# A two-block attention convolution on one core: group norm by single chunks, tile work of a pair's first image in the second attention, m2 and cv1's sums moved, first pair reordered

## The chip, the cores and the metric

The kernel runs on one core of a Trainium2 chip, in float32 throughout. The metric is the device time of one execution in microseconds (us), as the median of several runs. A profiled execution gives, for each engine, every instruction with its start and length. The engines are TensorE (PE in the profile; its weight loads are PEld), VectorE (DVE), ScalarE (ACT), GpSimd (POOL) and SyncE (SP), which issues most of the DMAs; GpSimd issues the others.

## The reference

Eight images of 512 channels and 32 x 32 pixels are normalised by groups of 16 channels and sent through a block with a residual around it. Cut to what matters:

```python
t = cbs(gn(x), cv1_w, cv1_bn, 0)            # 1x1 conv 512 -> 512, batch norm, silu
ys = [t[:, :256], t[:, 256:]]
for i in range(2):
    yi = ys[-1]
    z = cbs(yi, m_cv1_w[i], m_cv1_bn[i], 1)  # 3x3 conv 256 -> 256
    q, k, v = 1x1 conv of z, 256 -> 768      # 4 heads of 64, 1024 positions
    a = softmax(q . (k + rw + rh) / 8)
    z = silu(bn(1x1 conv of (a . v)))        # "m2" in the kernel
    ys.append(yi + z)
out = x + cbs(concat(ys), cv2_w, cv2_bn, 0)  # 1x1 conv 1024 -> 512
```

## The kernel before

The images go in four pairs (p = 0 to 3). Channels lie on the 128 partitions, so an image of 512 channels is four chunks of 128 x 1024. Within a pair the stages of block 0 are: the 3 x 3 conv of both images; projection of the first image to q, k, v; its attention (the *first attention*); a *middle* stage; projection of the second image; its attention (the *second attention*); m2 and the tiles of the second image. Block 1 follows with the same stages, and cv2 at the end of each image.

**The 3 x 3 conv** is a Winograd form. `tiles_in` (L453) makes its input side on VectorE from the padded image in `Y1` or `Y2`, in three steps i = 0, 1, 2, each of some 14 VectorE operations and two GpSimd memsets; a step's first tiles use the tag "acc", of which there are two buffers and which the attention's sums also use. The filters' side, `make_u` (L352), is made once at the start and in pair 0 (nine steps for each quarter of a filter, through `step_u`), stored to DRAM through GpSimd's queue and loaded back through SP's.

**Projection** is `project_strassen` (L737): seven products instead of eight, of sums of z (`first_sum`, t1 to t4), with the results combined on VectorE. PSUM has three "big" buffers and one "av" buffer. A `middle` function can be called inside it, in the kernel before after the fourth product; block 1 and pair 3 call m2 there.

**Attention** (`attention_fast`, L837) walks four groups of 8 key tiles in pairs of tiles: two logits matmul groups (`l_ps`, L860), two exps on ScalarE (`pt`, L864, six buffers of tag "pt"), sums of the exps on VectorE (`acc`, L878 and L880), and the products with v (`av_ps`, L894), which ScalarE (L901) and VectorE (L902) evict at a group's end. `sums`, `spread` and `scale` send the row sums through DRAM and multiply z by their reciprocals (L966). Foreign work is put in by `behind`, a table from (group, step) to a function; `hooks` fills it with `step_norm`, at the steps listed in `NORMS`, and `step_u`.

**Group norm** of the next pair's images (`group_norm`, L666) runs in such steps: statistics of two chunks, of the other two, the group means, then rstd, shift and all eight applications (L687, halves of a chunk) in one step.

**cv1** of the next pair's images is spread around the attentions as `begin`, `go_on`, `sums`, `rest(0)` to `rest(3)`, `adds`, `adds2`, `finish` and `keep`. In pair 0 (`direct`) it is a plain product by output chunk; later pairs use a Strassen form.

**The middle stage** (L1588) of pairs 0 to 2 is: cv1's second part and sums, `spread`, `scale`, m2 of the first image (which writes `Y2[0]`), the rest of cv1, then `tiles_in` of `Y2[0]` with results `v_new` put in tag "pt" and stored to DRAM by GpSimd, the next loads of x, and the projection of the second image. Pair 3 has no cv1: it calls m2 inside the projection and does the tile steps in the second attention, at the steps (0, 2), (1, 2) and (2, 2), with v_new in tag "x".

**The start** (L1372 to L1465) computes the norm of the first two images, filters (0, 1) and (0, 0), cv1 of both images, `make_sq` (sums for the projection's weights) and the tiles, with `issue_after` setting parts of the order. `load_bottleneck` (L174) loads m2's weights and makes r = rw + rh (`r_new`) on GpSimd for both blocks. Each engine executes its instructions in order; that order comes from a scheduler that honours `issue_after`.

Of the kernel before, what the change touches and what calls it, by code (L numbers as in the profile page):

```python
# [61 lines left out]
def kernel(  # L62
# [70 lines left out]

    xs = [load_x(act, 0, c, NX) for c in range(NX // 2)]
# [28 lines left out]

    xs_second = []
# [6 lines left out]
    m2_sb = const.tile([P, N, NM, C], F32, name="m2_sb")  # L171
    rw_sb = const.tile([P, N, NM, F], F32, name="rw_sb")
    rh_sb = const.tile([P, N, NM, F], F32, name="rh_sb")

    def load_bottleneck(n):
        raw = act.tile([P, NM, F], F32, tag="t", name="rw_raw", bufs=4)
        nc.sync.dma_start(raw, m_rw[n].rearrange("(k p) f -> p k f", p=P))
        nc.sync.dma_start(rh_sb[:, n], m_rh[n].rearrange("(k p) f -> p k f", p=P))
        nc.sync.dma_start(m2_sb[:, n], m_cv2_w[n].rearrange("(k p) o -> p k o", p=P))
        nc.gpsimd.tensor_copy(planes(rw_sb[:, n]), natural(raw))  # L180
        for c in range(NM):
            for half in range(NH):
                r = act.tile([P, ROWS, F], F32, tag="t", name="r_new", bufs=4)
                nc.gpsimd.tensor_tensor(
                    r, rw_sb[:, n, c].unsqueeze(1).to_broadcast([P, ROWS, F]),
                    rh_sb[:, n, c, ts(half, ROWS)].unsqueeze(2).to_broadcast([P, ROWS, F]), ALU.add,
                )
                nc.gpsimd.dma_start(r_dram[n][c][:, ts(half, HALF)], r.rearrange("p h w -> p (h w)"))
# [236 lines left out]
    def stages(act, small, ps_big, ps_av, n_pt):  # L425
# [219 lines left out]
        def group_norm_part(xts):  # L645
# [3 lines left out]
            for c in range(n):  # L649
                gn_stats(mv, c, xts[c])  # L650
# [15 lines left out]
        def group_norm(xts):  # L666

            mv = small.tile([P, NX, 2], F32, tag="mv", name="mv", bufs=2)

            def stats(cs):  # L670
                for c in cs:
                    gn_stats(mv, c, xts[c])

            stats(range(NX // 2))
            yield
            stats(range(NX // 2, NX))
            yield
# [5 lines left out]
            nc.gpsimd.tensor_scalar(shift, shift, -1.0, None, ALU.mult)  # L683
            for c in range(NX):
                for half in range(NH):
                    part = xts[c][:, ts(half, HALF)]
                    nc.scalar.activation(part, part, AF.Identity, scale=gr[:, c : c + 1], bias=shift[:, c : c + 1])  # L687
            yield
# [48 lines left out]
        def project_strassen(n, z, w, t, early=None, middle=None):  # L737
# [64 lines left out]
            if middle:  # L802
                middle()
# [3 lines left out]
            tt(u_v, ps_w[:, 0], u_v, ALU.add)  # L807
            ps_d = big()
# [617 lines left out]
    with tc.issue_after(last.ins), tc.issue_after(applied.ins):  # L1426
        norm = s.group_norm_part(xs_second)
# [3 lines left out]
    areas[0, 0, 0] = load_raw(0, 0, 0, Y2[0])  # L1431
    areas[0, 0, 1] = load_raw(0, 0, 1, Y2[1])
# [13 lines left out]
    for n in range(N):  # L1446
        load_bottleneck(n)
    scratch = act.tile([P, 4, HW], F32, tag="z", name="sq_new")
    flat = scratch.rearrange("p a b -> p (a b)")
    tiles = [flat[:, ts(k, 3 * C)] for k in range(NM)]  # L1450
    load_qkv(0, tiles)
    sums = [flat[:, 2 * 3 * C + j * 3 * P : 2 * 3 * C + (j + 1) * 3 * P].rearrange("p (w o) -> p w o", w=3) for j in range(4)]
    with tc.issue_after(made.ins):
        made = make_sq(0, tiles, sums)
# [4 lines left out]
    with tc.issue_after(made.ins):  # L1459
        ecs = [{}, {}]  # L1460
        for i in range(NI):
            for g in range(G):
                s.tiles_in(Y1[g], putter(vs, g), [i], ecs[g])
# [3 lines left out]
    for p in range(NP):  # L1467
# [23 lines left out]
        def next_cv1(which, xts, y1, b):  # L1491
# [3 lines left out]
            if direct:  # L1495
# [4 lines left out]
                    rest=lambda i: one(1 + i) if i in (1, 2) else None, adds=nothing, adds2=nothing, finish=nothing,  # L1500
# [46 lines left out]
        def hooks(norms, every=1):  # L1547
            calls = {}
            for g in range(NG):
                for at in range(4):  # L1550
                    key = (g, at) if at else g
                    calls[key] = [step_norm] if key in norms else []
                    if (4 * g + at) % every == 0:
                        calls[key].append(step_u)
            return {key: (lambda fs: lambda: [f() for f in fs])(fs) for key, fs in calls.items()}

        NORMS = (1, 2, (2, 2), 3)
# [14 lines left out]
        def put_away(i, cp):  # L1572
            tag, bufs = ("pt", 6) if more else ("x", NX)
            v_new[i, cp] = t = act.tile([P, 2, 2 * P], F32, tag=tag, name="v_new", bufs=bufs)
# [13 lines left out]
        if more:  # L1588
# [4 lines left out]
            nxt.rest(0)  # L1593
            end.scale()
            last = m2_a()
            for i in range(1, 4):
                nxt.rest(i)
            with tc.issue_after(last.ins):
                t = s.first_sum(z[:, :, 1])
                nxt.adds()  # L1600
# [5 lines left out]
            for i in range(2):  # L1606
                s.tiles_in(Y2[0], put_away, [i], ec)
                store(i)
            for _ in range(12):
                step_u()  # L1610
# [5 lines left out]
            s.tiles_in(Y2[0], put_away, [2], ec)  # L1616
            store(2)
        else:
            norm = None
            t = s.first_sum(z[:, :, 1])  # L1620

            def middle():
                end.spread()
                end.scale()
                m2_a()
                with tc.issue_after(s.silu_in[-1].ins):
                    s.table_of(AF.Exp)

            feed(units(1)[:6])
            qkv = s.project_strassen(  # L1630
                0, z[:, :, 1], take_blocks("sq", 0, 1, SQ_NAMES), t, early=end.sums, middle=middle
            )

            def tiles_later(i):
                s.tiles_in(Y2[0], put_away, [i], ec)
                store(i)
# [11 lines left out]
        behind = hooks(NORMS) | {NG: begin_cv1(1, Y1[1], ia + 3), NG + 1: lambda: nxt.go_on()}  # L1648
        if not more:
# [11 lines left out]
            behind |= {(i, 2): (lambda i: lambda: tiles_later(i))(i) for i in range(NI)}  # L1661
# [231 lines left out]
```

## Time and profile before

| What | us |
|---|---|
| median of 3 runs (2430.92 to 2432.46) | 2432.45 |
| profiled execution | 2428.35 |
| its span, first to last instruction | 2426.9 |
| TensorE busy | 2253.8 |
| VectorE busy | 1776.7 |
| ScalarE busy | 1100.2 |
| mean granted TensorE clock | 0.973 of full |

TensorE's first attention matmul starts at 163.55 us. The block 0 part of pair 0 lasts until 485.6 (conv of block 1 included), pair 1 starts its first attention at 786.7, pair 2 at 1368.6, pair 3 at 1950.9. A row of a timeline reads: start, length, engine, line and operation, output and inputs, shape, number of instructions, and in brackets the idle time of that engine before it with the instruction that ended the wait.

### The profile page before, as it was taken

To read this page: it belongs to the slowest core of one execution; us is meant where nothing else is said; L and a number is where in the kernel's file an instruction comes from. 1 tells how busy PE (TensorE), PEld (TensorE's weight loads), DVE (VectorE), ACT (ScalarE), POOL (GpSimd) and SP (SyncE) were. 2 spreads that over 40 slices of the span, in tenths; PEclk is the share of its full clock that TensorE was granted. 3 is DMA by queue.
4 is the path that set the end of the run, shared out by engine and by line. 5 is a ranking of instruction groups with operands and counts; after the bars stand their busy time and mean duration, and the time that the engine had idled before them with its cause. 6 is when DMAs were issued, how large, how long until landed. Compare 5 with 4: busy or idle time off the path is not lost.

```text
span 2426.9 us, 40682 instructions
## 1 busy us (share of the span) xinstructions
PE 2253.8 (93%) x16378; PEld 1092.5 (45%) x16378; DVE 1776.7 (73%) x2678; ACT 1100.2 (45%) x1341; POOL 214.7 (9%) x435
## 2 busy tenths in 40 slices
PE   6798788999999989999999998999999999999997
PEld 2462333734447343554346534373434734373433
DVE  7987585877857768786884858698685777797652
ACT  4245344365323655446522565535642355435532
POOL 5201110000021000000012001000002100000002
PEclk9899889999999999999999999999999999999999
DMA  8631623621257041443137414161215712251205
GB/s 309 243 125 67 239 76 96 242 91 59 57 154 246 17 161 49 162 128 97 32 87 225 143 58 152 59 215 54 88 45 131 254 36 71 83 178 35 75 17 137
DMA packets 137477, 290.89 MB, mean 120 GB/s; under 512 B 34656, under 2 KB 63824, under 8 KB 136256
## 3 DMA queue, kind: packets, MB, share of 16 engines
q1 hardware_dynamic: 108976, 201.29, 25.7%
q0 software_dynamic: 28304, 86.92, 11.7%
q8 instruction: 131, 2.15, 0.4%
q14 instruction: 66, 0.54, 0.1%
HBM read 216.97 MB, written 71.17 MB: 119 GB/s over the span
## 4 chain that ended last, share of the span: by engine, by line
PE 51%; DVE 21%; issue 17%; DMA 5%; ACT 4%; POOL 2%; SPq 0%; DVEq 0%; ACTq 0%; POOLq 0%
PE av_ps L894 12%; PE l_ps L860 12%; PE p_ps L750 5%; PE c L1111 5%; PE m_ps L1091 3%; PE c_new L1111 3%; PE ps L448 3%; DVE acc L880 3%; PE x_ps L1211 2%; PE c_ps L565 2%; DMA c_out<-in_x_dram 2%; PE pv_ps L756 2%; ACT x L687 1%; ACT pt L864 1%; DVE c_e L573 1%
## 5 line engine op out<-in xcount | busy, mean ns | idle before, releaser
L864 ACT ACTIVATE pt<-l_ps 128x1024 f32<-128x1024 f32 x512 | 495.9, 1022 | 373.6 <-PE l_ps L860 339.3
L880 DVE TENSOR_TENSOR acc<-acc,pt 128x1024 f32<-128x1024 f32 x384 | 469.8, 1223 | 128.7 <-ACT pt L864 104.5
L860 PE MATMUL l_ps<-q,kr 64*64 64x512 f32 x4096 | 494.2, 598 | 44.4 <-ACT pt L864 43.0
L894 PE MATMUL av_ps<-pt,vT 64*64 64x512 f32 x4096 | 500.1, 606 | 11.2 <-DVE z L902 7.6
L860 PEld LDWEIGHTS l_ps<-q,kr 64*64 64x64 f32 x4096 | 157.5, 134 | 316.8 <-issue 245.3
L894 PEld LDWEIGHTS av_ps<-pt,vT 64*64 64x64 f32 x4096 | 157.4, 136 | 300.0 <-issue 256.2
L565 PE MATMUL c_ps<-v_in,u 128*64 128x128 f32 x4320 | 239.9, 273 | 5.2 <-issue 2.7
L565 PEld LDWEIGHTS c_ps<-v_in,u 128*64 128x64 f32 x4320 | 235.8, 137 | 12.8 <-issue 12.8
L750 PE MATMUL p_ps<-t_z,sq 128*128 128x512 f32 x256 | 126.2, 609 | 7.6 <-DVE c_t L572 7.6
L1091 PE MATMUL m_ps<-z,m_sb 128*128 128x512 f32 x256 | 114.3, 599 | 7.9 <-DVE z L966 7.9
L750 PE MATMUL p_ps<-z,sq 128*128 128x512 f32 x192 | 97.9, 645 | 24.3 <-ACT u_z L784 14.9
L570 ACT COPY c_m<-c_ps 128x512 f32<-128x512 f32 x48 | 28.1, 586 | 174.8 <-PE c_ps L565 110.0
L878 DVE TENSOR_TENSOR acc<-pt 128x1024 f32<-128x1024 f32 x64 | 78.2, 1221 | 30.4 <-ACT pt L864 30.4
L966 DVE TENSOR_TENSOR z<-z,rs 128x512 f32<-128x512 f32 x64 | 44.1, 689 | 68.3 <-DMA rs<-r_dram 68.0
L429 ACT ACTIVATE t<-m_ps,bh,sh 128x512 f32<-128x512 f32 x64 | 46.9, 776 | 81.3 <-PE m_ps L1091 80.9
L1091 PEld LDWEIGHTS m_ps<-z,m_sb 128*128 128x128 f32 x256 | 48.7, 192 | 67.6 <-issue 57.2
L1161 POOL DMA_DIRECT2D c_out<-in_x_dram x56 | 49.6, 967 | 307.8 <-ACT c_out L429 303.2
L756 PE MATMUL pv_ps<-sq,z 128*128 128x128 f32 x384 | 54.1, 285 | 16.0 <-DVE z L902 8.2
L756 PEld LDWEIGHTS pv_ps<-sq,z 128*128 128x128 f32 x384 | 50.3, 196 | 40.2 <-DVE z L902 11.3
L750 PEld LDWEIGHTS p_ps<-z,sq 128*128 128x128 f32 x192 | 36.4, 204 | 67.9 <-issue 39.5
L750 PEld LDWEIGHTS p_ps<-t_z,sq 128*128 128x128 f32 x256 | 44.9, 195 | 42.3 <-issue 32.3
L902 DVE TENSOR_TENSOR z<-av_ps,z 128x512 f32<-128x512 f32 x64 | 44.1, 689 | 24.3 <-ACT z L901 24.3
(278 smaller groups left out, 3149.9 us busy)
## 6 DMA issues: line engine op xcount, KB each, us to landing
u<-u SPq DMA_DIRECT2D x135, 512.0 KB
sq<-sq SPq DMA_DIRECT2D x48, 384.0 KB
r_in<-r SPq DMA_DIRECT2D x32, 512.0 KB
rs<-r_dram SPq DMA_DIRECT2D x120, 128.0 KB
x<-in_x_dram SPq DMA_DIRECT2D x28, 512.0 KB
y_in<-y SPq DMA_DIRECT2D x28, 512.0 KB
c_out<-in_x_dram POOLq DMA_DIRECT2D x56, 256.0 KB, 5.3
out_dram<-c_out POOLq DMA_DIRECT2D x56, 256.0 KB, 3.2
```

The costliest lines, as they stand in the source:

```text
L448: last_product[0] = nc.tensor.matmul(ps[:, half, :], w_of(k), rhs_of(k, half), start=(k == begin), stop=(k == end))
L565: nc.tensor.matmul(to[o], us[cp][:, k, row, c, o], rhs, start=(k == 0), stop=(k == NM - 1),)
L750: nc.tensor.matmul(ps[:, o, :], w[:, o, :], rhs, start=not onto, stop=True, skip_group_check=onto)
L756: nc.tensor.matmul(v[:, ts(j, P)], rhs[:, ts(j, P)], w[:, 2, :], start=j == 0 and not onto, stop=True, skip_group_check=True,)
L860: nc.tensor.matmul(ps[kh * HD : (kh + 1) * HD, hd, :], kr[r, c, o : o + HD], q[r, c, ts(half, HALF)], start=True, stop=True,)
L864: exp = nc.scalar.activation(pt, ps, AF.Exp, scale=SCALE)
L878: return nc.vector.tensor_tensor(accs[g], pt[0], pt[1], ALU.add)
L880: ins = nc.vector.tensor_tensor(accs[g], accs[g], pt[i], ALU.add)
L894: nc.tensor.matmul(avs[g][hd * HD : (hd + 1) * HD, kh, :], vT[r, j, o : o + HD], pt[i][r, hd, :], start=(j == 0), stop=(j == NJ - 1),)
L1091: nc.tensor.matmul(pss[oc][:, half, :], m2_sb[:, n, k, ts(oc, P)], ao[:, k, ts(half, HALF)], start=(k == 0), stop=(k == NM - 1),)
L1111: nc.tensor.matmul(ps[:, o, :], w[:, k, ts(o, P)], rhs[part][:, c], start=(k == 0 and not onto), stop=(k == KB - 1), skip_group_check=onto,)
L1161: nc.gpsimd.dma_start(t, rows_of(x, i, at), accum_op=ALU.add)
```

## The change

- `group_norm` gives one chunk per step, for statistics and for application, and applies a whole chunk in one activation. `NORMS` has ten steps.
- The tiles of a pair's first image move for all pairs to the second attention, at (0, 2), (1, 2), (2, 2), with v_new in tag "t" (four buffers).
- `middle` is called after the fifth product (s2) of `project_strassen`.
- In the middle stage of pairs 1 and 2 `rest(1)` and `adds` come before m2. Pair 0 goes pair 3's way: m2 and two output chunks of cv1 inside the projection.
- At the start, the second image's statistics come from ScalarE (`stats_by_act`), the filter (0, 0) is loaded earlier into the tile of z (`load_taps`), r of block 0 is made early and that of block 1 after pair 0's projection, the qkv weights go to `Y2`, `make_sq` comes after the tiles, and the tiles' order changes.

```diff
-    def load_bottleneck(n):
+    def load_r(n):
         raw = act.tile([P, NM, F], F32, tag="t", name="rw_raw", bufs=4)
         nc.sync.dma_start(raw, m_rw[n].rearrange("(k p) f -> p k f", p=P))
         nc.sync.dma_start(rh_sb[:, n], m_rh[n].rearrange("(k p) f -> p k f", p=P))
+        return raw
+    rw_raw = load_r(0)
+    taps = act.tile([P, NM, 2 * HW], F32, tag="z", name="taps")
+    areas[0, 0, 0] = load_taps(0, 0, 0, taps[:, 0])
     xs_second = []
...
+    areas[0, 0, 1] = load_taps(0, 0, 1, taps[:, 1])
+    def load_m2(n):
         nc.sync.dma_start(m2_sb[:, n], m_cv2_w[n].rearrange("(k p) o -> p k o", p=P))
+    def make_r(n, raw):
         nc.gpsimd.tensor_copy(planes(rw_sb[:, n]), natural(raw))
...
+        def stats_by_act(mv, xts):
+            n = len(xts)
...
+            def each(func, to, **kw):
+                for c in range(n):
+                    bias = {k: v[:, c : c + 1] for k, v in kw.items()}
+                    junk = act.tile([P, HW], F32, tag="acc", name="junk", bufs=2)
+                    nc.scalar.activation(junk, xts[c], func, accum_out=to[:, c : c + 1], **bias)
+            each(AF.Identity, total)
+            nc.vector.tensor_scalar(mean, total, -1.0 / HW, None, ALU.mult)
+            each(AF.Square, square, bias=mean)
+            nc.vector.tensor_scalar(mv[:, :, 0], total, 1.0 / HW, None, ALU.mult)
+            nc.vector.tensor_scalar(mv[:, :, 1], square, 1.0 / HW, None, ALU.mult)
...
         def group_norm(xts):
             mv = small.tile([P, NX, 2], F32, tag="mv", name="mv", bufs=2)
-            def stats(cs):
-                for c in cs:
-                    gn_stats(mv, c, xts[c])
-            stats(range(NX // 2))
-            yield
-            stats(range(NX // 2, NX))
-            yield
+            for c in range(NX):
+                gn_stats(mv, c, xts[c])
+                yield
...
+            yield
             for c in range(NX):
-                for half in range(NH):
-                    part = xts[c][:, ts(half, HALF)]
-                    nc.scalar.activation(part, part, AF.Identity, scale=gr[:, c : c + 1], bias=shift[:, c : c + 1])
-            yield
+                nc.scalar.activation(xts[c], xts[c], AF.Identity, scale=gr[:, c : c + 1], bias=shift[:, c : c + 1])
+                yield
...
-            if middle:
-                middle()
             ps_c, ps_w = big(), big()
             product(ps_c, ps_w[:, 0], w["s2"], t2)
             tt(u, ps_c, u, ALU.add)
             tt(u_v, ps_w[:, 0], u_v, ALU.add)
+            if middle:
+                middle()
...
-        norm = s.group_norm_part(xs_second)
+        norm = s.group_norm_part(xs_second, by_act=True)
...
-    areas[0, 0, 0] = load_raw(0, 0, 0, Y2[0])
-    areas[0, 0, 1] = load_raw(0, 0, 1, Y2[1])
+    make_r(0, rw_raw)
...
-    with tc.issue_after(made.ins):
-        made = make_sq(0, tiles, sums)
...
-        for i in range(NI):
-            for g in range(G):
-                s.tiles_in(Y1[g], putter(vs, g), [i], ecs[g])
+        for g, i in ((0, 0), (0, 1), (1, 0), (1, 1), (0, 2), (1, 2)):
+            last = s.tiles_in(Y1[g], putter(vs, g), [i], ecs[g])
+    with tc.issue_after(last.ins):
+        make_sq(0, tiles, sums)
...
-        NORMS = (1, 2, (2, 2), 3)
+        NORMS = ((0, 3), (1, 1), (1, 3), (2, 1), (2, 2), (2, 3), 3, (3, 1), (3, 2), (3, 3))
...
-            tag, bufs = ("pt", 6) if more else ("x", NX)
-            v_new[i, cp] = t = act.tile([P, 2, 2 * P], F32, tag=tag, name="v_new", bufs=bufs)
+            v_new[i, cp] = t = act.tile([P, 2, 2 * P], F32, tag="t", name="v_new", bufs=4)
...
-        if more:
+        if more and not direct:
             end.sums()
             nxt.go_on()
             nxt.sums()
             end.spread()
             nxt.rest(0)
+            nxt.rest(1)
+            nxt.adds()
             end.scale()
             last = m2_a()
-            for i in range(1, 4):
+            for i in range(2, 4):
                 nxt.rest(i)
...
-            for i in range(2):
-                s.tiles_in(Y2[0], put_away, [i], ec)
-                store(i)
-            for _ in range(12):
-                step_u()
...
-            s.tiles_in(Y2[0], put_away, [2], ec)
-            store(2)
         else:
             t = s.first_sum(z[:, :, 1])
+            if more:
+                nxt.go_on()
             def middle():
                 end.spread()
                 end.scale()
                 m2_a()
+                if more:
+                    for i in range(2, 4):
+                        nxt.rest(i)
+                    nxt.keep()
...
+            if more:
+                make_r(1, load_r(1))
+                for _ in range(12):
+                    step_u()
+                xs = [load_x(act, ia + 3, c, NX) for c in range(NX)]
+                norm = s.group_norm(xs)
...
-        behind = hooks(NORMS) | {NG: begin_cv1(1, Y1[1], ia + 3), NG + 1: lambda: nxt.go_on()}
+        extra = {i: (lambda i: lambda: tiles_later(i))(i) for i in range(NI)}
+        behind = hooks(NORMS, 1, {(0, 2): extra[0], (1, 2): extra[1], (2, 2): extra[2]}) | {
+            NG: begin_cv1(1, Y1[1], ia + 3), NG + 1: lambda: nxt.go_on()
+        }
```

## The prediction

> **What bounds the kernel now.** I read the page's busy shares first, then TensorE's timeline for every idle gap, then ScalarE's and VectorE's timelines at the large gaps, and last the busy time by stage. TensorE is the bound, with 2253.8 us busy of 2426.9. The change leaves the number of its matmuls alone, so it can only win from the 173 us in which TensorE idles and from the slow matmuls behind a long gap.
>
> ```profile
> PE 2253.8 (93%) x16378; PEld 1092.5 (45%) x16378; DVE 1776.7 (73%) x2678; ACT 1100.2 (45%) x1341; POOL 214.7 (9%) x435
> ```
>
> TensorE's timeline, in the brackets the idle time before a row and who ended it: end of the tile work at the start, m2 of pair 0, projection of pair 0's second image, end of a first attention (pair 1), projection of pair 1's second image, second attention of pair 3.
>
> ```profile
> 118.53 9.32 PE L565 MATMUL c_ps<-v_in,u_new 128*64 128x128 f32 x128 [7.73 <-ACT c_m L570]
> ...
> 269.99 3.51 PE L1091 MATMUL m_ps<-z,m_sb 128*128 128x512 f32 x4 [7.89 <-DVE z L966]
> ...
> 299.25 5.95 PE L750 MATMUL p_ps<-z,sq 128*128 128x512 f32 x8 [7.38 <-ACT u_z L784]
> ...
> 845.10 1.98 PE L860 MATMUL l_ps<-q,kr 64*64 64x512 f32 x8 [5.10 <-ACT pt L864]
> ...
> 902.72 6.29 PE L750 MATMUL p_ps<-z,sq 128*128 128x512 f32 x8 [4.07 <-ACT u_z L784]
> ...
> 2071.75 3.58 PE L894 MATMUL av_ps<-pt,vT 64*64 64x512 f32 x16 [3.20 <-DVE z L902]
> ```
>
> ScalarE's timeline names the causes behind two of them: eight norm activations in one run ahead of the exps, and a copy that waits for the DMA of v_new to free a "pt" buffer.
>
> ```profile
> 838.39 5.75 ACT L687 ACTIVATE x<-x,shift,gr 128x512 f32<-128x512 f32 x8 [3.84 <-POOL shift L683]
> ...
> 901.66 1.01 ACT L784 COPY u_z<-p_ps 128x1024 f32<-128x1024 f32 x1 [5.00 <-DMA v<-v_new]
> ```
>
> Busy time by stage: window, length, then PE, PEld, DVE, ACT, POOL, the granted clock. In order: start up to the first attention; pair 0's first attention, between, second attention; the same three of pair 1; then first and second attention of pair 3.
>
> ```profile
> 0.00:163.50 163.50, 121.12 (x812) 77.02 (x812) 137.61 (x297) 55.71 (x85) 49.77 (x102) 0.92 0.72 250
> 163.50:237.00 73.50, 61.64 (x547) 20.98 (x545) 59.73 (x90) 43.67 (x56) 6.17 (x12) 0.93 0.11 36
> 237.00:311.20 74.20, 58.29 (x176) 28.15 (x172) 44.28 (x89) 23.87 (x33) 15.48 (x34) 0.91 0.65 229
> 311.20:395.50 84.30, 65.53 (x547) 21.18 (x545) 64.67 (x103) 43.01 (x56) 9.57 (x18) 0.90 0.24 79
> 786.70:852.00 65.30, 60.20 (x546) 21.48 (x545) 51.01 (x67) 42.07 (x50) 1.47 (x3) 0.95 0.09 24
> 852.00:915.00 63.00, 55.06 (x164) 27.44 (x164) 40.47 (x65) 30.42 (x33) 6.23 (x16) 0.92 0.48 169
> 915.00:981.40 66.40, 60.70 (x547) 21.44 (x545) 52.44 (x71) 40.69 (x48) 2.54 (x5) 0.95 0.12 37
> 1950.90:2008.40 57.50, 57.50 (x539) 19.76 (x537) 44.16 (x47) 35.75 (x41) 0.00 (x0) 1.00 0.09 26
> 2035.50:2098.40 62.90, 59.15 (x538) 20.15 (x537) 58.25 (x80) 35.21 (x40) 5.54 (x15) 0.97 0.20 68
> ```
>
> An attention without a stall takes 57.4 us (57.5 in pair 3). In pair 3's second attention, which already holds the tile work, VectorE is busy 58.25 us and the stage takes 62.9.
>
> **What the Trainium skill says.** "TensorE: Matmul & The Clock Gate", Part 1 (the HAM clock gate): an idle window of about 3.4 us puts the array at half clock until it has been busy as long. The trace agrees: the eight-row L750 group after the 4.07 us gap takes 6.29 us, against 3.70 elsewhere. The same page, "Architectural detail": ScalarE's and VectorE's queues are strictly first in, first out. The trace agrees: exps stand behind the norm run. "SBUF — State Buffer", Terms: VectorE and GpSimd lock a shared port pair for a whole instruction. The trace agrees: two 0.42 us VectorE operations take 2.75 and 2.48 us at 58.2 and 65.3 us, beside GpSimd's r_new.
>
> **The change, part by part.** All sums are against the profiled execution (2428.35 us; span 2426.9). It lies 4.1 us under the median of 2432.45, and I carry that over.
>
> 1. *Start.* VectorE is the path: it starts tiles at 76.1 and its last v_in ends at 117.8. Gone ahead of that: eight bn_stats and four aggregates, 33.4 to 40.4 less the first tap sum (0.55) and its stall (1.4), 5.0; make_sq's four sums, 2.0 (now beside the conv); the two stalls from the second block's r_new, 4.4; the wait for taps, 1.0. Added: three small scalings, 0.6, and perhaps a third r_new stall, 2. Net 10. ScalarE gets eight activations of 1024: taking the 1.02 us of an exp of that size, 8.2 us, which pushes its first silu from 33.4 to about 42. That is covered: x_second's norm needs its statistics about 41 instead of going through VectorE at 47.5, so it is applied near 49 (56.5 before), and the first silu is needed only at tile work near 66. In the new tile order conv waits for three tile steps instead of two, but then has its second row ready, and VectorE stays busy into the projection, so I take VectorE's lead. On SP's queue rw, rh and 576 KB of taps move ahead of x_second, 2 us at the stage's 300 GB/s (0.6 MB); x_second was not waited for at 33.4 and is now wanted at 30.5. load_qkv now waits for the areas in Y2, free when the last taps of (0, 1, 1) are used near 41; make_sq's seven stores leave GpSimd during conv, near 110, and the projection wants them near 131. Gain 10, bounds 5 and 14.
>
> 2. *Norm in a first attention.* Four applies of about 1.0 us, two and two in ScalarE's built order, in place of 5.75 in one run. A pair step has 3.43 us of TensorE and 1.94 of exps. Following pair 1 from 831: shift ready about 834, two applies to 835.9, exps to 837.8, two applies to 840.0, exps to 842, so the last av ends about 845.5 instead of 852. 1.7 us of stall remain. Pair 1 gains 6, pair 2 (64.5 us before) 5. Pair 0: 73.5 falls to 64, as VectorE has 59.7 to do there: 9.5, bounds 6 and 12. Statistics one chunk at a time cost VectorE the same.
>
> 3. *Between the attentions, pairs 1 and 2.* 63.0 us before; matmuls at full clock 53.6 (3.7 + 0.6 + 10.6 + 7.0 + 10.5 + 21.4, stage rows of TensorE). The tile steps (18 us of VectorE) leave, v_new leaves the "pt" buffers, so u_z waits for no DMA: the gaps of 3.20, 0.68 and 4.07 and the 2.6 of slow clock go. m2 comes later behind rest(0) and rest(1), which gives the sums more cover. What is late next is ScalarE's silus of cv1, about 1.5 us. Gain 8 and 7.5.
>
> 4. *Between, pair 0.* 74.2 before, matmuls 57. The u_z gap (7.38) and its slow clock (2.2) go. m2 now stands in the projection, after 11.3 us of products and 3.5 of its own first half. From s_ps to the scaled z took 25 us here (244.05 to 269.24); 6.4 of that were s_row behind silus, so about 19 stay, and SP now has four 512 KB loads between s_dram and rs instead of three. So 4 to 5 us of m2's wait remain. Gain 12, bounds 7 and 16.
>
> 5. *Second attentions, pairs 0 to 2.* This is where it pays. Three tile steps of 6.2, 5.6 and 6.2 us (issue intervals of VectorE's rows) join norm statistics and acc sums. Pair 3 has VectorE busy from 2035.5 to the last sum at 2102.3, 66.8 us, which ended TensorE's attention 4 us earlier, at 2098.4. Adding 6.1 of norm (four chunks of 1.3, small ones 0.9) gives 73, so the attention ends near 69; and all four applies stand in one run before the last exps there, 3.8 us, partly beside VectorE's lag. Against 66.4 I take +3 each for pairs 1 and 2. In pair 0 VectorE goes from 64.7 to 80, against a stage of 84.3 that already had 20 idle on VectorE, and the second r_new's four operations and stores on GpSimd come in with their port stalls: +3. The nine v_new stores (0.54 us of GpSimd each) now stand ahead of the norm's pow and shift on that queue; the last of them waits for the third tile step, behind which VectorE's gr stands anyway, so they cost nothing more. Bounds for the three together: 0 and +28.
>
> 6. *m2 after the s2 product* (five projections, four of the second block and pair 3's). Nothing waited on m2 before, so nothing is won. ps_d now waits for ps_w and for m2's silus: 8.0 us of silu chain against 7.0 of m2 and 1.7 of products beside it, and the exp table's load comes 2.6 us later. +0.5 each, +2.5, bounds 0 and +8.
>
> Sum: -10 -9.5 -11 -15.5 -12 +9 +2.5 = -46.5. Profiled span 2380, median 2386.
>
> **Rivals.**
> - *A, the cover holds further* (15%): VectorE's lateness in second attentions falls beside cv1's first products, as in pair 3 (item 5 at 0), and the start gains 14: -59.5, 2373. For it: pair 3 lost only 5.5 with the whole tile work. Against: pair 3 has no norm.
> - *B, less is won* (19%): the tile blocks and u_new copies hold exps as at 327 us, so item 5 costs 20; ScalarE's late silus hold the start at 6; m2 in pair 0 still waits 8 (-8): -46.5 + 11 + 4 + 4, 2405. For it: pair 0's ScalarE idles 5.8 and 7.1 us behind u_new.
> - *C, slower* (5%): a tile block in VectorE's queue holds the eviction of av_ps, of which there is one buffer. Measured once: 3.20 plus 1.7 of slow clock. With a block of 6.2, a statistics chunk of 1.4 and that clock, 9.3 each, nine blocks are 84, against 55.5 won elsewhere: about 2461. It decides from 18.5 us lost per second attention. Against: that eviction stands ahead of most of a tile block in the built order, and pair 3 lost 3.2 at one block of three.
> - *The change misses its aim* (1%): the one run of applies stays a single wait because GpSimd's shift is late, and the DMA chain sets both middles: within 5 us of before.
>
> **The numbers.** My forecast has 60%: 2386. Its own bounds, the independent items together, reach some 15 us to each side. A lies inside; to take in B and half of its far side I go from 2360 to 2413. A measurement of this kernel tells about 0.2%, 4.9 us: faster 0.94, same 0.01, slower 0.05.
>
> **What would show it.** Step 1: first attention begins near 153 instead of 163.5. Step 2: L687's form becomes 128x1024 x4 in groups of two, the gap before the last logits under 2 us. Step 3: no ScalarE wait on the DMA of v_new; the middle of pairs 1 and 2 near 55. Step 4: m2 of pair 0 waits under 6. Step 5: VectorE near full in second attentions of 68 to 70, about 87 in pair 0. Step 6: L806's stage unchanged within 1 us. I am wrong if second attentions exceed 75, or if ScalarE's statistics delay conv's first matmul past 94.

## The result and the profile after

The changed kernel takes 2417.47 us (median of 4 runs, 2412.48 to 2418.39) against 2432.05 for the kernel before on the same chip: a ratio of 0.9937 with a 95% interval of 0.9919 to 0.9954. It is faster by 14.6 us where 46.5 were forecast, and the time lies 4.5 us above the stated range. The span of the profiled execution fell from 2426.9 to 2415.7 us, by 11.2.

The stages are cut where TensorE's first and last attention matmuls stand in its timeline. Lengths in us:

| Stage | Before | After | Forecast | Measured |
|---|---|---|---|---|
| start, up to the first attention | 163.6 | 158.1 | -10 | -5.5 |
| first attention, pairs 0, 1, 2 | 73.5, 65.3, 64.5 | 68.3, 60.0, 60.0 | -9.5, -6, -5 | -5.2, -5.3, -4.5 |
| middle, pair 0 | 74.2 | 65.7 | -12 | -8.5 |
| middle, pairs 1, 2 | 63.0, 62.5 | 50.3, 50.3 | -8, -7.5 | -12.7, -12.2 |
| second attention, pairs 0, 1, 2 | 84.3, 66.4, 66.3 | 96.8, 78.5, 77.8 | +3, +3, +3 | +12.5, +12.1, +11.5 |
| all else (step 6 is in it) | | | +2.5 | +6.6 |

The rows add up to the 11.2 of the span. What was to be won in front of the second attentions was won, 53.9 us of 58 forecast; the second attentions gave back 36.1 where 9 were priced. Of the 6.6 in the last row, step 6 has 1.1, the stage behind pair 0's second attention 1.5 and pair 3's second attention 1.3; the rest is spread over many stages.

Busy time by stage of the changed kernel (window, length, then PE, PEld, DVE, ACT, POOL, the granted clock): the middle of pair 0; then first attention, middle and second attention of pair 1; then the second attention of pair 3.

```profile
226.40:292.10 65.70, 58.49 (x174) 29.38 (x174) 28.42 (x60) 25.38 (x36) 18.47 (x31) 0.90 0.61 218
781.60:841.60 60.00, 57.98 (x546) 20.18 (x545) 48.37 (x64) 39.59 (x45) 1.46 (x3) 1.00 0.07 21
841.60:891.90 50.30, 50.30 (x168) 25.09 (x168) 25.95 (x35) 30.89 (x35) 1.70 (x3) 1.00 0.54 182
891.90:970.40 78.50, 63.70 (x546) 21.72 (x545) 68.87 (x103) 39.70 (x44) 7.74 (x18) 0.90 0.17 58
2021.70:2085.90 64.20, 60.27 (x538) 19.99 (x537) 59.10 (x81) 35.29 (x40) 5.53 (x15) 0.95 0.19 65
```

The middle of pair 1 has no gap left: TensorE is busy 50.30 of 50.30 us. The second attention has VectorE busy 68.9 us, but it lasts 78.5. So VectorE idles there too, for almost 10 us, and its amount of work alone doesn't explain the length.

TensorE's timeline of that second attention names what it waits for:

```profile
926.53 0.74 PE L942 MATMUL s_ps<-acc,ones 128*32 128x256 f32 x8 [2.80 <-DVE acc L911]
930.36 3.61 PE L925 MATMUL av_ps<-pt,vT 64*64 64x512 f32 x16 [3.10 <-DVE z L933]
...
943.09 0.22 PE L638 MATMUL gm_ps<-mv,gmat 64*64 64x4 f32 x2 [2.25 <-DVE mv L632]
...
966.66 3.69 PE L925 MATMUL av_ps<-pt,vT 64*64 64x512 f32 x16 [5.92 <-ACT pt L895]
```

Four waits: the row sums wait for VectorE's lag; av_ps waits for an eviction (L933) that stands behind a tile block; the norm's little group-mean matmul stands in TensorE's queue and waits for the last statistics; and the last products wait for exps. The 16 matmuls of L925 take 3.6 and 3.7 us after the second and the fourth gap instead of 1.90. "TensorE: Matmul & The Clock Gate" of the Trainium skill, Part 1, has the array at half clock after an idle window of about 3.4 us. The gap of 5.92 us agrees with that; the gap of 3.10, which follows one of 2.80 with 0.74 us of work between, is shorter than the page's window, and here the measurement decides. The last wait is made by three engines in a row, in their timelines:

```profile
957.72 0.15 DVE L657 TENSOR_SCALAR gr<-gv_ps 128x4 f32<-128x4 f32 x1
...
960.49 0.54 POOL L715 TENSOR_SCALAR shift<-shift 128x4 f32<-128x4 f32 x1
...
961.06 4.63 ACT L718 ACTIVATE x<-x,shift,gr 128x1024 f32<-128x1024 f32 x4 [5.03 <-POOL shift L715]
```

TensorE's timeline has gv_ps done by 948.6. VectorE turns it into gr only at 957.72, because the rest of the third tile block, with one sum of exps in it, stands ahead of it; GpSimd's shift follows, and ScalarE waits 5.03 us for it and then puts four applications ahead of the last two exps.

In pair 0 the last wait is the same and longer, 9.48 us, and there is another of almost that length: exps stand on ScalarE behind a filter's copy, and that waits for sums which VectorE reaches late, behind a statistics step and in among the rows of the second tile block. The third line is the last wait.

```profile
339.91 0.42 ACT L391 ACTIVATE u_new<-ypad 128x256 f32<-128x256 f32 x1 [11.20 <-DVE ypad L377]
...
341.29 1.08 PE L942 MATMUL s_ps<-acc,ones 128*32 128x256 f32 x8 [9.39 <-ACT pt L895]
...
385.19 3.69 PE L925 MATMUL av_ps<-pt,vT 64*64 64x512 f32 x16 [9.48 <-ACT pt L895]
```

### The profile page after: what moved, and what is told of

Its sections match the earlier page's. It is cut to its first block, busy times and chain, and to the rows that moved or that the text cites. A ratio compares the mean times of both kernels' runs of the same rounds, so it can differ in the third digit from the quotient of the medians.

```text
span 2415.7 us, 40666 instructions
## 1 busy us (share of the span) xinstructions
PE 2247.7 (93%) x16378; PEld 1085.3 (45%) x16378; DVE 1767.8 (73%) x2669; ACT 1098.9 (45%) x1333; POOL 220.7 (9%) x435
## 4 chain that ended last, share of the span: by engine, by line
PE 49%; DVE 19%; issue 18%; DMA 5%; ACT 3%; POOL 2%; SPq 0%; DVEq 0%; ACTq 0%; POOLq 0%
PE av_ps L925 10%; PE l_ps L891 10%; PE c L1142 5%; PE p_ps L781 4%; PE m_ps L1122 4%; PE x_ps L1242 3%; PE c_new L1142 3%; DVE acc L911 3%; PE ps L464 2%; PE pv_ps L787 2%; PE c_ps L581 2%; DMA c_out<-in_x_dram 2%; ACT pt L895 1%; DVE acc L909 1%; PE p_ps L787 1%
## 5 line engine op out<-in xcount | busy, mean ns | idle before, releaser
L895 ACT ACTIVATE pt<-l_ps 128x1024 f32<-128x1024 f32 x512 | 495.8, 1022 | 383.8 <-PE l_ps L891 357.6
L925 PE MATMUL av_ps<-pt,vT 64*64 64x512 f32 x4096 | 501.2, 607 | 35.0 <-ACT pt L895 21.3
L891 PE MATMUL l_ps<-q,kr 64*64 64x512 f32 x4096 | 494.4, 598 | 15.0 <-ACT pt L895 12.7
L925 PEld LDWEIGHTS av_ps<-pt,vT 64*64 64x64 f32 x4096 | 156.0, 136 | 319.2 <-issue 246.4
L781 PE MATMUL p_ps<-z,sq 128*128 128x512 f32 x192 | 91.9, 605 | 9.6 <-ACT z L445 9.6
L499 POOL MEMSET w_rows<- 128x32 f32 x48 | 7.9, 165 | 645.8 <-PE s_ps L942 454.7
L787 PEld LDWEIGHTS pv_ps<-sq,z 128*128 128x128 f32 x384 | 51.1, 199 | 33.2 <-issue 11.2
L933 DVE TENSOR_TENSOR z<-av_ps,z 128x512 f32<-128x512 f32 x64 | 43.9, 686 | 26.6 <-ACT z L932 26.6
```

Of the source, the lines that this page charges most:

```text
L781: nc.tensor.matmul(ps[:, o, :], w[:, o, :], rhs, start=not onto, stop=True, skip_group_check=onto)
L787: nc.tensor.matmul(v[:, ts(j, P)], rhs[:, ts(j, P)], w[:, 2, :], start=j == 0 and not onto, stop=True, skip_group_check=True,)
L891: nc.tensor.matmul(ps[kh * HD : (kh + 1) * HD, hd, :], kr[r, c, o : o + HD], q[r, c, ts(half, HALF)], start=True, stop=True,)
L895: exp = nc.scalar.activation(pt, ps, AF.Exp, scale=SCALE)
L925: nc.tensor.matmul(avs[g][hd * HD : (hd + 1) * HD, kh, :], vT[r, j, o : o + HD], pt[i][r, hd, :], start=(j == 0), stop=(j == NJ - 1),)
```

## The experiments

All times are medians; a stage's length is from the run's one profiled execution. Each ratio is to the kernel before as it was run beside the variant.

### Norm steps earlier in the second attentions

```diff
-        behind = hooks(NORMS, 1, {...}) | {
+        NORMS_B = ((0, 1), (0, 3), 1, (1, 1), (1, 3), 2, (2, 1), (2, 3), (3, 1), (3, 2))
+        behind = hooks(NORMS_B, 1, {...}) | {
```

> The changed kernel with one edit: in the second attentions the same ten norm steps come earlier (statistics at (0,1), (0,3), 1, (1,1); mean at (1,3), rstd at 2, applications at (2,1), (2,3), (3,1), (3,2)); no work is added or removed. Theory 'order': the 12 us that a second attention lost come from instructions waiting behind each other (the group mean in TensorE's queue behind the last statistics, the four applications behind a shift that waits for VectorE's third tile block). Then the second attentions of pairs 1 and 2 fall from 78 us to about 66, pair 0's from 97 to about 88, and the kernel takes about 2385 us. Theory 'volume': VectorE has 69 us of work there and sets the length in any order; then they stay at 75 to 80 and the kernel stays at 2412 to 2420.

Measured: 2398.26 us, ratio to before 0.9863 (0.9848 to 0.9878). The second attentions take 86.2, 72.0 and 72.2 us instead of 96.8, 78.5 and 77.8. No work was removed, so these 10.6, 6.5 and 5.6 us were order alone; in pairs 1 and 2 the next stage grew by 1.3 and 1.6, so that 5.2 and 4.0 stay. The rest did not go: in pair 1 the group mean and the step behind it now wait longer than in the changed kernel, as TensorE's timeline shows.

```profile
914.98 0.27 PE L638 MATMUL gm_ps<-mv,gmat 64*64 64x4 f32 x2 [4.26 <-DVE mv L632]
...
927.93 0.22 PE L638 MATMUL gv_ps<-dev,gmat 64*64 64x4 f32 x2 [4.24 <-DVE dev L650]
```

So "order" holds for about half of the loss in pairs 1 and 2 and for most of it in pair 0, and the forecast of 66 for pairs 1 and 2 fails. "Volume" fails too: all three stages moved, and in pair 1's 72.0 us VectorE is busy 63.4.

### The third tile step later

```diff
-{(0, 2): extra[0], (1, 2): extra[1], (2, 2): extra[2]}
+{(0, 2): extra[0], (1, 2): extra[1], (3, 2): extra[2]}
```

> The changed kernel with one edit: the third tile step of the second attentions at (3,2) instead of (2,2), so that VectorE computes gr ahead of that block. Theory 'order': the last wait of a second attention (5.9 us of idle TensorE and 1.8 of half clock) is the applications waiting for gr behind the block; the wait before the last products falls under 2, and the second attentions of pairs 1 and 2 take 69 to 72 instead of 78 (pair 0 88 to 90): about 2395 us. Rival 'the block is paid anyway': the block comes right behind the attention, where m2 and cv1 wait for VectorE, and the next stage (87 us) grows by 4 or more; or the wait stays above 4.

Measured: 2397.59 us, 0.987 (0.9854 to 0.9885). The second attentions take 87.8, 70.9 and 69.7 us. In pair 1, gr runs at 938.58, shift keeps ScalarE waiting 1.39 us instead of 5.03, the applications fall apart into two and two, and the last gap is 1.08 us:

```profile
940.50 2.37 ACT L718 ACTIVATE x<-x,shift,gr 128x1024 f32<-128x1024 f32 x2 [1.39 <-POOL shift L715]
```

The next stage grew by 2.8 and 3.7 us in pairs 1 and 2, since the block stands there now, so about 4.6 of the 7.9 won per attention stay. The theory's 69 to 72 came in pairs 1 and 2, and the next stage grew by less than the 4 us that the rival asked for. So the wait behind the third block was real and is priced here.

### The tile steps of pairs 1 and 2 back in the middle, v_new in tag t

```diff
+            for i in range(2):
+                s.tiles_in(Y2[0], put_away, [i], ec)
+                store(i)
             xs = [load_x(act, ia + 3, c, NX) for c in range(NX)]
...
             qkv = s.project_strassen(0, z[:, :, 1], take_blocks("sq", 0, 1, SQ_NAMES), t)
+            s.tiles_in(Y2[0], put_away, [2], ec)
+            store(2)
...
-        behind = hooks(NORMS, 1, {...}) | {
+        late = {...} if direct or not more else {}
+        behind = hooks(NORMS, 1, late) | {
```

> The changed kernel with the tile steps of pairs 1 and 2 back in the middle stage, at the places of the kernel before, but with v_new kept in tag t. Theory 'cover': the middle has VectorE idle for half its time and only the wait of u_z for the store of v_new was dear, so the middle of pairs 1 and 2 goes from 50.3 to about 55 and the second attention from 78 to about 65, which is 8 us won per pair: about 2401. Rival 'tiles cost the same anywhere': the middle goes to 60 or more, the two stages together stay within 3 us of 129, and the kernel stays at 2413 to 2423.

Measured: 2395.43 us, 0.9852 (0.9837 to 0.9867). The middle takes 55.1 and 55.0 us, the second attention 61.3 and 61.3. The same three steps cost 4.7 us in the middle and, in pair 1, 17.2 in the attention. With the norm alone in it, the attention's own waits are small:

```profile
932.07 1.95 PE L925 MATMUL av_ps<-pt,vT 64*64 64x512 f32 x16 [0.45 <-DVE z L933]
...
950.28 2.00 PE L891 MATMUL l_ps<-q,kr 64*64 64x512 f32 x16 [1.57 <-ACT pt L895]
```

"Cover" holds, by more than was expected. Together with pair 3, whose second attention has tile steps and no norm, this splits the loss of a second attention over its 57.4 us. The rows are TensorE's idle time by what it waited for, then what its matmuls lost by running slowly (its busy time over 57.4):

| us | Tile steps alone (pair 3, after) | Norm alone (pair 1, this run) | Both (pair 1, after) |
|---|---|---|---|
| row sums (L942) | 0.55 | 1.29 | 2.80 |
| eviction of av_ps (L933) | 3.20 | 0.45 | 3.10 |
| group mean (L638) | none | none | 2.25 |
| late exps at the end (L895) | none | 1.57 | 5.92 |
| shorter gaps | 0.18 | none | 0.74 |
| slow matmuls | 2.9 | 0.6 | 6.3 |
| length over 57.4 | 6.8 | 3.9 | 21.1 |

Both together cost not the sum of the two but 10.4 more. The eviction behind a tile block has no part in that: it waits as long with the tile steps alone. What is new are the late exps, the group mean and longer waits of the row sums: in all 7.6 us more idle time than the two columns before have together. The slow matmuls add 2.8.

The slow matmuls are partly luck of an execution. Pair 3's second attention has the same gap of 3.20 us in most runs. After it the 16 matmuls take 3.69 us in the changed kernel, but 1.95 in three runs, where the stage lasts 61.7 us instead of 64.2:

```profile
2037.74 1.95 PE L925 MATMUL av_ps<-pt,vT 64*64 64x512 f32 x16 [3.20 <-DVE z L933]
```

(This line is from the run with tile steps in pair 0's middle, below.) So the 6.8 are between 4.4 and 6.9, and the 10.4 is uncertain by as much; its 7.6 us of idle time are not touched. A difference of 2 us between two profiles at such a place need not come from the edit.

### The kernel before, with v_new in tag t

```diff
-            tag, bufs = ("pt", 6) if more else ("x", NX)
+            tag, bufs = ("t", 4) if more else ("x", NX)
```

> The kernel before with one edit: v_new of pairs 0 to 2 in tag t (four buffers) instead of tag pt. Theory: the waits of u_z for the store of v_new are the whole of what that stage loses, so the middles of pairs 1 and 2 go from 63 to about 55, as in the changed kernel with its tile steps there, and pair 0's from 74 to 65 to 68: about 2407 us. Rival: the order of m2 and cv1's sums did as much, and the middle stays at 59 or more.

Measured: 2413.8 us, 0.9932 (0.992 to 0.9944): this one line wins as much as the whole change. The middle of pairs 1 and 2 falls to 55.3 and 56.8 us, so the theory holds there, and ScalarE's copy of u_z no longer waits:

```profile
884.90 1.06 ACT L784 COPY u_z<-p_ps 128x1024 f32<-128x1024 f32 x1
```

In pair 0 the middle stays at 73.4. There the wait only changed its place: u_zv is in tag t too, and now its copy waits for a buffer that the store frees, so that TensorE waits 4.38 us there. In pair 1 that copy waits as well, 3.76 us, but TensorE only 1.23 for it.

```profile
295.70 0.59 ACT L785 COPY u_zv<-pv_ps 128x512 f32<-128x512 f32 x1 [5.69 <-DMA v<-v_new]
```

### The norm of the kernel before

> The changed kernel with the norm of the kernel before: statistics of two chunks in a step, all applications as eight half chunks in one step, at 1, 2, (2,2), 3. If single chunks won what the first attentions lost less (5.2, 5.3 and 4.5 us), these go back to about 73, 65 and 64.5 us; the second attentions, in which the applications stood in one run anyway, move by less than 3 each: about 2432. Rival: in the second attentions the earlier mean of the old places (rstd at 3 but mean at (2,2)) makes the norm cheaper there, by 4 or more each, and the kernel stays within 4 us of 2417.

The edit gives back `NORMS = (1, 2, (2, 2), 3)`, two statistics steps and eight half-chunk applications in one step. Measured: 2434.86 us, 1.0017 (1.001 to 1.0023), a little slower than the kernel before. The first attentions take 72.2, 64.9 and 64.2 us, so single chunks, applied whole, are worth 3.9, 4.9 and 4.2 there. The second attentions take 96.7, 80.4 and 80.1, so the places of the old norm are no cheaper with tile steps around them. Without the single chunks the change would not have won anything.

### make_sq's sums on GpSimd

```diff
-        last = sums_of(blocks, sums)
+        last = sums_of(blocks, sums, nc.gpsimd.tensor_tensor if n == 0 else tt)
```

> The changed kernel with the four sums of make_sq for block 0 on GpSimd instead of VectorE. Theory: at the start VectorE is the path from the tiles through the conv, so that the 2.2 us of these sums, moved behind the tiles, were still paid, and so was the filter work that stood with them (1.6 us and a wait of 1.5 for its load); then the first attention begins at about 154 to 156 instead of 158.1. Rival: from the conv on TensorE and ScalarE set the pace; then it begins at 158 within 0.5. The total moves by the same amount, 2413 to 2417.

Measured: 2426.48 us, 0.9981 (0.9974 to 0.9989), and the first attention begins at 166.1, 8 us later. The experiment does not answer its question: the order now drew a sum of the next filter in among the tile work (perhaps because buffers come free earlier, which is not shown), where it waits at the head of VectorE's queue for its load.

```profile
84.19 0.56 DVE L375 TENSOR_TENSOR ypad<-ypad 128x384 f32<-128x384 f32 x1 [11.34 <-DMA ypad<-in_m_cv_w_dram]
```

TensorE's first conv matmul begins at 102.3 us instead of 89.0. So the run shows only that a wait of VectorE at the start is paid in TensorE's time.

### The next filter's sums held back

```diff
+                with tc.issue_after(s.first_sums[-1].ins):
-                for _ in range(12):
-                    step_u()
+                    for _ in range(12):
+                        step_u()
```

(`first_sums` collects the instruction of `first_sum`, which runs behind the first attention.)

> The changed kernel with one edit: the three sums of the next filter (L375 to L377), which the order had drawn forward into the first conv, are held until after the first attention. They take 1.65 us of VectorE and 1.5 of waiting for their load there. Theory: VectorE is the path through the first conv, so that the first attention begins at about 155 us instead of 158.1. Rival: TensorE and ScalarE set the pace behind the tiles, and it begins at 158 within 0.5. Everything after it moves by less than 1 us per stage; total 2414 or 2417.

Measured: 2407.9 us, 0.9908 (0.9892 to 0.9923). The first attention begins at 155.6 instead of 158.1, as the theory said. Profiles of the same start vary: in eight executions without this edit (the run with make_sq on GpSimd left out) it begins between 158.1 and 160.4, in the three with it, two of them below, between 155.6 and 156.8. Pair 0's middle also became shorter, 62.7 against 65.7, which was not expected. The trace shows how: the filter copy that stands ahead of cv1's first two silus on ScalarE comes 5.4 us sooner in the stage, and a gap of TensorE of 3.40 us at the row sums is gone. A later gap grew from 3.67 to 5.51, so idle time fell by only 0.7; the other 2.3 are matmuls that ran faster.

### Tile steps in the middle for pairs 0 and 3 too

The run with both edits (early norm everywhere, tile steps of pairs 1 and 2 in the middle):

> The changed kernel with both edits: norm steps early in every second attention, and the tile steps of pairs 1 and 2 back in the middle with v_new in tag t (pairs 0 and 3 keep theirs in the second attention). If the two causes are separate, pair 0's second attention is as with the early norm (86 us), the middle of pairs 1 and 2 is 55, and their second attention, 61.3 with the late norm, falls to 58 to 60: about 2381 us. Rival: both edits remove the same waits, the second attentions of pairs 1 and 2 stay at 61, and only pair 0 gains: about 2385.

Measured: 2387.52 us, 0.9826 (0.9813 to 0.984). Pair 0's second attention takes 86.3, but those of pairs 1 and 2 take 63.0, 1.7 more than with the late norm. The early places help only where tile blocks stand in the same attention, and neither the theory's 58 to 60 nor the rival's 61 came.

> As the run with both edits, and pair 0's tile steps in its middle too (two inside the projection after m2, the third behind it). Theory 'cover': VectorE has 28 us to do in the 65 us of pair 0's middle, so 18 us of tile steps cost about 5 there and take about 10 from its second attention (86 to 76): about 2376 us. Rival: behind m2 only two of seven products are left (6 us of TensorE), so the tile steps stand in front of the sums that make q, k and v; the middle goes from 65 to 74 or more and nothing is won: 2380 to 2386.

> As the run before it, and the same for pair 3, whose middle has no cv1 (27 us). Theory 'cover ends where the stage is short': there VectorE has no idle time for 18 us, the middle of pair 3 goes from 27 to 33 or more, the second attention from 64.3 to 57.5, so that pair 3 wins at most 2 us. Rival 'tiles are cheap in any middle': the middle grows by less than 4 and pair 3 wins 3 or more.

Measured: 2395.25 us, 0.9859 (0.9843 to 0.9874), and 2405.23 us, 0.9903 (0.9888 to 0.9918): both slower than the run without. The middles hardly grew (67.4 in pair 0, 26.7 in pair 3), but pair 0's second attention went from 86.3 to 92.8 and pair 3's from 63.1 to 74.5. In pair 3 VectorE's timeline shows a block of the tile work between the sums that make q, k and v, and TensorE's shows the wait:

```profile
2012.99 1.21 DVE L497 TENSOR_TENSOR w_g<-ypad 128x1024 f32<-128x1024 f32 x1
2014.12 0.67 DVE L854 TENSOR_TENSOR vT<-vT,pv_ps 128x512 f32<-128x512 f32 x1
...
2014.85 3.69 PE L925 MATMUL av_ps<-pt,vT 64*64 64x512 f32 x16 [8.13 <-DVE vT L854]
```

In pair 3 the edit was expected to win little because VectorE would have no idle time. It does have it, busy only 11.2 of the middle's 26.7 us; but m2's result comes late, so that the blocks stand in front of the sums, and the loss shows in the attention's first steps rather than in the middle.

The theory for pair 0 falls, and its rival's cause is there: a tile block waits 4.85 us in VectorE's queue for the store of v_new, ahead of the sums that make q and k, and TensorE waits 4.34 for them.

```profile
296.12 0.43 DVE L530 SCALAR_TENSOR_TENSOR v_new<-w_d 128x256 f32<-128x256 f32 x1 [4.85 <-DMA v<-v_new]
...
326.50 1.99 PE L925 MATMUL av_ps<-pt,vT 64*64 64x512 f32 x8 [9.81 <-ACT pt L895]
```

The larger gap, 9.81 us, comes later: exps stand behind a filter copy that waits for VectorE. How much of the loss belongs to each was not separated.

### The best parts together

Tile steps of pairs 1 and 2 in the middle, the early norm in pair 0's second attention alone, the filter sums held back.

> The changed kernel with three edits that won alone: tile steps of pairs 1 and 2 in the middle with v_new in tag t and the norm at its late places, the norm early in pair 0's second attention only, and the next filter's sums held until after the first attention. If the parts add up: 2395 less 10 (pair 0's second attention 96 to 86) less 3 (start), about 2382 us. Rival: the held filter sums come back in pair 0's middle or second attention, which then takes 89 or more, and the kernel is at 2385 to 2390.

Measured: 2373.78 us, 0.9764 (0.975 to 0.9778), the fastest of all; by the two ratios that is some 42 us below the changed kernel. The parts more than add up: pair 0's second attention takes 86.0, and pair 1 has its two stages as in the run with the middle alone. Pair 0's middle, 62.2, was not counted in the forecast; the rest of the difference to 2382 was not followed. Windows: pair 0's second attention, pair 1's middle and second attention.

```profile
286.50:372.50 86.00, 66.08 (x546) 21.89 (x545) 76.95 (x134) 41.91 (x52) 15.04 (x31) 0.90 0.30 108
825.80:880.80 55.00, 51.15 (x164) 25.20 (x165) 39.87 (x63) 31.24 (x35) 5.65 (x15) 1.00 0.57 190
880.80:942.10 61.30, 57.99 (x546) 20.07 (x545) 51.72 (x72) 39.27 (x44) 3.08 (x6) 1.00 0.13 38
```

> As the run with the three parts, but in pair 0's second attention the statistics stand early, the mean one step later (at 2), rstd at (2,2), applications at 3, (3,1), (3,2), (3,3). Theory: what remains dear there is the group mean in TensorE's queue waiting for statistics (5.3 us with the early places); with a step more between them this falls below 2 and the attention takes 82 to 84. Rival: the statistics are late because VectorE has too much to do, the wait moves along, and the attention stays at 86 or goes back towards 96.

Measured: 2380.07 us, 0.9791 (0.9778 to 0.9805). Pair 0's second attention takes 93.4: the rival holds. The group mean's wait is gone, as the theory wanted, but two others have come in its place:

```profile
333.61 1.08 PE L944 MATMUL s_ps<-acc,ones 128*32 128x256 f32 x8 [6.09 <-DVE acc L913]
339.07 3.38 PE L927 MATMUL av_ps<-pt,vT 64*64 64x512 f32 x16 [4.38 <-DVE z L935]
```

The edit moves the mean, the rstd and the applications all to later places, so it doesn't say which of them made it worse.

## Why the prediction was wrong

The step that failed is step 5, the second attentions: 36.1 us were lost where the text has +9, and the changed kernel misses the forecast of 2386 by 31.

**Step 5.** It added VectorE's work, 66.8 and 6.1, and concluded that "the attention ends near 69". That is close to what the parts give when they stand alone: 57.4, 6.8 for tile steps and 3.9 for the norm make 68.1. What it left out are 10.4 us that come only when both stand in one attention: 7.6 us of waits between engines and 2.8 of slow matmuls. It had the largest of these waits in hand and priced it too low. That gr stands behind the third tile block was used to show that the stores cost nothing more, not that the applications are held by it (5.03 us of ScalarE); and the run of four applications before the last exps was seen, but put "partly beside VectorE's lag", where TensorE waits 5.92 us. The group mean as a matmul that waits in TensorE's own queue (2.25 us) was not thought of. The eviction behind a tile block, kept for rival C, was already in pair 3's 62.9. That the order of steps is the cause of a large part is shown by two runs: in pairs 1 and 2 the norm earlier won 6.5 and 5.6 us, 5.2 and 4.0 after what it cost in the next stage, and the third block later 4.6 on average after that cost. No run that keeps both in one attention removes all the new waits, so the share beyond these figures rests on the traces. In pair 0, which lost 12.5, the norm earlier won 10.6.

**Step 3.** Right in its mechanism, mis-sized: 12.7 and 12.2 instead of 8 and 7.5. Tag t alone wins 7.8 and 5.7, and the tile steps leaving another 4.7; the order of m2 and of cv1's sums has at most the small rest, 0.2 and 1.8. The full-clock sum of 53.6, whose terms add up to 53.8, was too high, since the projection takes 18.6 us without waits and not 21.4, and the silus' 1.5 us did not appear.

**Step 2.** Pairs 1 and 2 within 0.7 us. An application takes 1.23 us, not 1.0: in "ScalarE: Activation LUTs" of the Trainium skill, section What ACT_TABLE_LOAD costs, an activation costs 186 ns, 0.833 ns an element and 93 ns for each scale or bias that is read from a column of 128 x 1. With both, an estimate from that page is 1225 ns; the trace agrees, with 1223 to 1255 ns and a median of 1230. Pair 0 kept waits of TensorE behind filter copies (1.86 us), an eviction (2.37) and the applications (2.49) and won 5.2 of 9.5.

**Step 4.** m2's wait vanished altogether, but two others of 3.40 and 3.67 us appeared in its place, for cv1's silus. These stand in ScalarE's queue behind copies of a filter, which wait for VectorE. Rows of ScalarE and TensorE in order of time:

```profile
241.15 0.42 ACT L391 ACTIVATE u_new<-ypad 128x256 f32<-128x256 f32 x1 [4.81 <-DVE ypad L381]
...
245.44 1.08 PE L942 MATMUL s_ps<-acc,ones 128*32 128x256 f32 x8 [3.40 <-ACT y_half L445]
...
249.28 0.42 ACT L391 ACTIVATE u_new<-ypad 128x256 f32<-128x256 f32 x1 [2.70 <-DVE ypad L377]
...
252.20 3.78 PE L781 MATMUL p_ps<-t_z,sq 128*128 128x512 f32 x4 [3.67 <-ACT y_half L445]
```

The gap at u_z was gone, as forecast; the run with tag t alone shows that in pair 0 this took the move of the tile steps out of the stage, since with them there the store holds u_zv in the new tag.

**Step 1.** VectorE's lead was as forecast: tiles begin at 65.3 instead of 76.1, and the last v_in ends at 107.7 instead of 117.8. Almost half of it, 4.6 us, was lost behind that, in the conv, where VectorE is still the path. "Now beside the conv" was wrong: make_sq's sums (2.2 us between 107.6 and 110.1) stand ahead of the conv's own sums, and three sums of a later filter, with a wait for their load, did too. Holding the latter back won 2.5 us. The share of make_sq was not isolated.

**Step 6.** The stages that it speaks of moved by -0.5, +1.7, -0.1, +0.3 and -0.3 us: small, as said.

**Rivals.** None came as a whole. B, 2405, is the nearest. Its start (6 us won) and its middle of pair 0 (8) came out at 5.5 and 8.5, though not through the late silus at the start and the wait of m2 that it names; its third term has the right reason, exps held by tile blocks and filter copies, but 20 us where 36.1 came. C has one of the four waits, the eviction, and its deciding point, 18.5 us per second attention, was not reached at 12. A has the second attentions at nothing.

## What to carry to other kernels

Two pieces of work that fit into a stage one at a time need not fit together. Here the sum of busy times missed the length because short, early-needed instructions (a group mean, the input of a reciprocal root) stood behind long blocks in in-order queues; so list for each such instruction what is ahead of it and who waits behind it. The same tile steps cost 4.7 us in a middle stage, where VectorE is busy half of the time, and 17.2 in the attention behind it. But their input must be ready early enough there: in pair 3, where it comes late, they cost some 10 to 13 us more in the earlier stage's queue than in the attention. A buffer freed by a store is a wait like any other: one tag changed in the old kernel won as much as the whole change.

## What was not expected of the hardware

An activation that also accumulates is followed by a read of the accumulator. In the start's statistics on ScalarE each 128 x 1024 activation took 1.04 us (1.13 with a bias column) and each read 0.19, but the activations began only 1.04 us apart (1.14): a read lay beside the end of one and the beginning of the next. The two groups of four took 4.26 and 4.62 us.

A gap of TensorE that is followed by slow matmuls in one execution need not be so in another: after 3.20 us of idle time at the same place of the same code, 16 matmuls took between 1.95 and 3.69 us, and after 2.37 or 2.38 us, in pair 0's first attention, between 1.95 and 3.52.
